# Layer 1's convolution along w: six quarter-width products for four columns in place of four half-width products for two, and another order of the first stage's end

## The chip, the cores and the metric

The kernel runs on one core of one Trainium2 chip, a single launch. The metric is the device time of the whole launch in microseconds. The core's engines work at the same time and wait for each other through semaphores: TensorE (PE, matrix products; PEld is its loading of weights), VectorE (DVE), ScalarE (ACT), GpSimd (POOL) and SyncE (SP, here only the issue of DMAs). Each engine does its instructions in the order in which the program gave them to it.

## The reference

A batch of 8192 images of 8 channels, 16 x 16 pixels, goes through four residual layers, each on a group-normalised input (four groups of two channels, no affine part):

```python
x = x + L0(gn(x))   # a dense map 2048 -> 2048 in tensor-train form, rank 8, plus bias
x = x + L1(gn(x))   # 3x3 convolution, padding 1, plus bias; batch norm over all images; relu
x = x + L2(gn(x))   # 3x3 convolution of a quantised input (+-127, scale from the maximum over everything)
x = x + L3(gn(x))   # 3x3 convolution with binarised weights, edge padding
```

What matters here is layer 1's convolution. For an output column w it is the sum over three taps k of g_k applied to input column w + k - 1. Each g_k is a 128 x 128 matrix, since channels and rows of the image (8 x 16) lie on the 128 partitions and the taps along h are built into a banded matrix.

## The kernel before, in words

**Tiles and stages.** An image batch is cut into NT = 64 tiles of P = 128 images. A tile is 128 partitions (channel, row) by 2048 elements (image, column), 1 MB in float32. There are three stages: the first does layer 0, the norm behind it and layer 1's convolution, the second layer 1's batch norm, relu and residual and the statistics of layer 2, the third layers 2 and 3. The change touches the first stage alone.

**A step.** The first stage is a loop of 256 steps; step n is quarter q = n mod 4 (32 images, 512 columns) of tile t = n div 4. `main(t, q, ...)` does layer 0's main product of the quarter: eight products `po<-u,core` of 512 columns that accumulate in one PSUM buffer, and then DVE's eviction `xs<-po`, which adds the result to x. Between the eight products (at r = 0 to 7) it calls the work that a dictionary `steps` lists for that r, in the order in which it was put in:

- r = 0 and r = 4: `expand` for the next quarter, 16 small products `pu<-w,xn` and ACT's copy `u<-pu` of 2048 elements. There is one `pu` buffer and two `u`.
- r = 1: `conv1_output` of the convolution done at the end of the step before, then `conv1_input` of the one that is done at the end of this step. The convolution runs LAG = 6 steps behind the main product.
- by the quarter: q = 0, `norm_sums(t - 1)` and at r = 4 ACT's squares for a coming tile; q = 1, `norm_stats(t - 1)` at r = 1, and at r = 4 `norm_spread` and `norm_apply` of t - 1; q = 2, `norm_b_sums` and `norm_b_stats`; q = 3, `add_bias` (POOL, 4.5 us) and `norm_b_spread`, `norm_b_apply`.

After `main`, `conv1` does the products of the convolution. So PE's order in a step is `pu`, half of `po`, `pu`, the other half of `po`, `pm`, `pc`.

**The norm chain.** `norm_stats` is a few small DVE instructions (the last is `mv<-mv,sq_a`), and then one on POOL, `mv<-mv,mhalf`, which takes the power -1/2. `norm_spread` is DVE's transpose `stat<-mv`; `norm_apply` is four DVE instructions of 1024 elements that write `x1n`, the normalised input of the convolution, with a zero column on either side.

**The convolution.** Per quarter, with d0 to d3 the four columns under two outputs, `conv1_input` makes d0 - d2 and d1 - d3 (one POOL instruction of 512 elements), d1 + d2 and d2 - d1 (two of 256). `conv1` does four products of 256 columns into `pm` and `pc`, and ACT copies the first half of `pm`, with the bias, into `m`. `conv1_output` makes the two output columns in `y` with three DVE instructions, and `conv1_stats` takes their mean and variance. `conv1_direct` does the last tile with three products of 512 columns a quarter.

**Buffers.** `po`, `pm` and `pc` go round three PSUM buffers with one tag ("mm"), in this order, one each per step. So a step's `po` writes the buffer of the step before's `po`, which `xs<-po` must have read. `v`, the convolution's input, has two buffers.

**Order.** The order on each engine is that of the program (`InOrder`, line 33, through which all of these instructions are recorded; they all bear line 43 in the profile, and are told apart by the names of what they write).

Of the kernel before, what the change touches and what calls it, by code (L numbers as in the profile page):

```python
# [8 lines left out]
F32 = mybir.dt.float32  # L9
# [3 lines left out]
AF = mybir.ActivationFunctionType  # L13
ALU = mybir.AluOpType
# [4 lines left out]
P = 128  # L19
C, H, W = 8, 16, 16  # L20
# [33 lines left out]
def tile_net(ctx: ExitStack, tc: tile.TileContext, xb, xt_in, pack0, pack1, out):  # L54
# [80 lines left out]
    def late_constants(late):  # L135

        w = load_pack(pack1, PACK1, late, "w1")
        yield "load"

        def band(wr, sh, dtype, name):  # L140

            acc = late.tile([P, 3 * C, H], F32, name=f"acc_{name}", tag="acc")
            b = (const1 if name == "1" else const).tile([P, 3, CH], dtype, name=f"band_{name}", tag=f"band_{name}")
            bv = b.rearrange("p k (c h) -> p (k c) h", c=C)
            wr = wr.rearrange("p (k n) -> p k n", k=3)
            for kh in range(3):
                wv = wr[:, kh, :].unsqueeze(2).to_broadcast([P, 3 * C, H])
                mv = sh[:, kh:kh + H].unsqueeze(1).to_broadcast([P, 3 * C, H])
                if kh == 0:
                    dve.tensor_tensor(acc, wv, mv, ALU.mult)  # L150
                    continue
                tmp = late.tile([P, 3 * C, H], F32, name=f"tmp_{name}_{kh}", tag="tmp")
                dve.tensor_tensor(tmp, wv, mv, ALU.mult)
                dve.tensor_tensor(bv if kh == 2 else acc, acc, tmp, ALU.add)
            L[f"band{name}"] = b

        for k in ("gamma", "beta", "bias2", "bias3"):
            L[k] = const.tile([P, 1], F32, name=k)
            dve.tensor_copy(L[k], w[k])

        L["grp"] = grp = blocks(32, 1.0 / 512, "grp")
        b1 = L["b1"] = const.tile([P, 1], F32, name="b1")
        dve.tensor_reduce(b1, w["linb"], AX.X, ALU.add)
        band(w["w1"], shz, F32, "1")

        g0, g1, g2 = (L["band1"][:, k] for k in range(3))
        fast = L["fast1"] = const1.tile([P, 4, CH], F32, name="fast1")
        dve.tensor_tensor(fast[:, 0], g0, g2, ALU.add)
        for k, op in ((1, ALU.add), (2, ALU.subtract)):
            dve.tensor_tensor(fast[:, k], fast[:, 0], g1, op)  # L170
            dve.tensor_scalar(fast[:, k], fast[:, k], 0.5, None, ALU.mult)
        dve.tensor_copy(fast[:, 0], g0)
        dve.tensor_scalar(fast[:, 3], g2, -1.0, None, ALU.mult)
        yield "layer 1"
        L["avg16"] = square_blocks(16, 1.0 / (16 * NT), "avg16")


        w2max = const.tile([P, 1], F32, name="w2max")
        dve.tensor_reduce(w2max, w["w2all"], AX.X, ALU.max, apply_absolute_value=True)
        sw = L["sw"] = const.tile([P, 1], F32, name="sw")  # L180
        dve.reciprocal(sw, w2max)
        dve.tensor_scalar(sw, sw, 127.0, None, ALU.mult)
        wr2 = w["w2"]
        dve.tensor_scalar(wr2, wr2, sw, MAGIC, ALU.mult, ALU.add)
        dve.tensor_scalar(wr2, wr2, MAGIC, 127.0, ALU.subtract, ALU.min)
        dve.tensor_scalar(wr2, wr2, -127.0, None, ALU.max)
        yield "layer 2"
        band(wr2, shz, BF16, "2")
        yield "band 2"


        dve.tensor_copy(she[:, 1:H + 1], shz[:, 1:H + 1])
        dve.tensor_copy(she[:, 0:1], shz[:, 1:2])
        dve.tensor_copy(she[:, H + 1:H + 2], shz[:, H:H + 1])
        wr3 = w["w3"]
        mean3 = L["mean3"] = const.tile([P, C], F32, name="mean3")
        dve.tensor_reduce(mean3, w["w3all"].rearrange("p (o n) -> p o n", o=C), AX.X, ALU.add,
                          apply_absolute_value=True)
        dve.tensor_scalar(mean3, mean3, 1.0 / (C * 9), None, ALU.mult)
        own = blocks(16, 1.0, "own")  # L200
        dve.tensor_tensor(own, own, mean3, ALU.mult)
        scale3 = L["scale3"] = const.tile([P, 1], F32, name="scale3")
        dve.tensor_reduce(scale3, own, AX.X, ALU.add)
        pos3 = late.tile([P, 9 * C], F32, name="pos3")
        dve.tensor_scalar(pos3, wr3, 0.0, None, ALU.is_gt)
        dve.tensor_scalar(wr3, wr3, 0.0, None, ALU.is_lt)
        dve.tensor_tensor(wr3, pos3, wr3, ALU.subtract)
        yield "layer 3"
        band(wr3, she, F32, "3")
        sign3 = L["sign3"] = const.tile([P, 3, CH], F32R, name="sign3")  # L210
        dve.tensor_copy(sign3, L["band3"])
        yield "band 3"

        wsum = L["wsum"] = const.tile([P, 2, 32], F32, name="wsum")
        dve.memset(wsum, 0.0)
        dve.tensor_copy(wsum[:, 0, 0:G], grp)
        dve.tensor_copy(wsum[:, 1, G:2 * G], grp)
        mod32 = const.tile([P, 32], F32, name="mod32")  # L220
        dve.tensor_reduce(mod32, ident.rearrange("p (q j) -> p j q", j=32), AX.X, ALU.add)
        quarter = L["quarter"] = blocks(32, 1.0, "quarter")
        gpad = L["gpad"] = const.tile([P, NQ, 32], F32, name="gpad")
        dve.memset(gpad, 0.0)
        dve.tensor_copy(gpad[:, :, 0:G], quarter.unsqueeze(1).to_broadcast([P, NQ, G]))
        for k, name in enumerate(("sel0", "sel1", "corr")):

            t = L[name] = const.tile([P, CH], F32, name=name)
            dve.tensor_copy(t.rearrange("p (g n) -> p g n", g=G),
                            mod32[:, G * k:G * k + G].unsqueeze(2).to_broadcast([P, G, CH // G]))  # L230
        yield "statistics"
# [16 lines left out]
    def samples(t):  # L248
        return t.rearrange("p (b w) -> p b w", w=W)
# [29 lines left out]
    with first as s:  # L279
# [112 lines left out]

        def conv1_input(t, q):
            x = x1n[t % 2][:, q * QS:(q + 1) * QS]
            v = wk.tile([P, 2, BANK], F32, name=f"v_{t}_{q}", tag="v")
            d, v12 = (v[:, i].rearrange("p (k b j) -> p k b j", k=2, j=W // 2) for i in range(2))
            d1, d2 = x[:, :, 1:W + 1:2], x[:, :, 2:W + 2:2]
            pool.tensor_tensor(d.rearrange("p k b j -> p b j k"),  # L400
                               *(x[:, :, i:i + W].rearrange("p b (j k) -> p b j k", k=2) for i in (0, 2)), ALU.subtract)
            pool.tensor_tensor(v12[:, 0], d1, d2, ALU.add)
            pool.tensor_tensor(v12[:, 1], d2, d1, ALU.subtract)
            T[t]["v", q] = d, v12

        def conv1(t, q):
            d, v12 = T[t].pop(("v", q))
            pm, po = (ps_m.tile([P, 2, BANK // 2], F32, name=f"{n}_{t}_{q}", tag="mm") for n in ("pm", "pc"))
            for ps, v, weights in ((pm, v12, (1, 2)), (po, d, (0, 3))):
                for k in range(2):  # L410
                    pe.matmul(ps[:, k], L["fast1"][:, weights[k]], v[:, k].rearrange("p b j -> p (b j)"),
                              start=True, stop=True)
            m1 = wk.tile([P, BANK // 2], F32, name=f"m1_{t}_{q}", tag="m1")
            act.activation(m1, pm[:, 0], AF.Identity, bias=L["b1"], scale=1.0)
            T[t]["m", q] = m1, pm, po

        def conv1_direct(t, q):

# [18 lines left out]
        def conv1_output(t, q):  # L437
            if q == 0:
                conv1_start(t)
            m1, pm, po = T[t].pop(("m", q))  # L440
            y = T[t]["y"][:, q * BANK:(q + 1) * BANK]
            pairs = [a.rearrange("p (b j) -> p b j", j=W // 2) for a in (m1, pm[:, 1])]
            for k, op in ((0, ALU.add), (1, ALU.subtract)):
                dve.tensor_tensor(samples(y)[:, :, k:W:2], *pairs, op)
            y3 = y.rearrange("p (n k) -> p n k", k=2)
            dve.tensor_tensor(y3, y3, po.rearrange("p k n -> p n k"), ALU.add)
            conv1_stats(t, q)

        def quarter_of(n, lag):
# [96 lines left out]
        norm_sums(t, NQ - 1)  # L546
        if NT > STAY + 2:
            load2(STAY + 2)
        conv1_input(t - 1, 3)
        norm_stats(t)  # L550
        conv1_output(t - 1, 2)
        conv1(t - 1, 3)
        norm_spread(t)
        conv1_start(t)
        for h in range(2):
            norm_apply(t, [h])
            for q in (2 * h, 2 * h + 1):
                conv1_direct(t, q)
            if h == 0:
                conv1_output(t - 1, 3)  # L560
        for q in range(NQ):
            conv1_stats(t, q)

# [410 lines left out]
```

## Time and profile before

| what | value |
|---|---|
| median of 3 runs | 4120.65 us (4120.42 to 4121.55) |
| the profiled execution's own time | 4119.56 us |
| its span, first to last instruction | 4117.4 us |
| PE, PEld busy | 3874.6 us (94%), 2022.6 us (49%) |
| DVE, ACT, POOL busy | 3223.0 us (78%), 2147.3 us (52%), 2047.1 us (50%) |
| mean granted clock of PE | 0.962 |
| 1000 to 2000 us: PE, DVE, ACT, POOL busy | 1000.0, 736.8, 460.9, 338.3 us |

Busy is the time in which an engine had an instruction under way. A product of float32 stands in the trace as two records, so four products of a quarter are eight records of `pm` and `pc`. The last row is a stretch in the middle of the first stage, which ends near 2900 us. Idle time is put down to the engine and the tile that ended it. The granted clock is the share of TensorE's full speed that the chip's throttle let it have.

### The profile page before, as it was taken

To read this page: it belongs to the slowest core of one execution; us is meant where nothing else is said; L and a number is where in the kernel's file an instruction comes from. 1 tells how busy PE (TensorE), PEld (TensorE's weight loads), DVE (VectorE), ACT (ScalarE), POOL (GpSimd) and SP (SyncE) were. 2 spreads that over 40 slices of the span, in tenths; PEclk is the share of its full clock that TensorE was granted. 3 is DMA by queue.
4 is the path that set the end of the run, shared out by engine and by line. 5 is a ranking of instruction groups with operands and counts; after the bars stand their busy time and mean duration, and the time that the engine had idled before them with its cause. 6 is when DMAs were issued, how large, how long until landed. Compare 5 with 4: busy or idle time off the path is not lost.

```text
span 4117.4 us, 50426 instructions
## 1 busy us (share of the span) xinstructions
PE 3874.6 (94%) x19362; PEld 2022.6 (49%) x19362; DVE 3223.0 (78%) x5040; ACT 2147.3 (52%) x1670; POOL 2047.1 (50%) x1350
## 2 busy tenths in 40 slices
PE   7999999999999999999999999999666559999999
PEld 4555555555555555555555555555222125555555
DVE  8777777777777777777777777776799889999997
ACT  4444444444444444444444444443565557777776
POOL 2433333333333333333333333332788759999999
PEclk9999999999999999999999999999777679999999
DMA  3222222222222222222222222211799914444432
GB/s 132 103 82 103 95 91 103 91 94 95 90 103 84 101 103 82 103 100 85 103 92 93 100 87 100 89 75 70 310 425 425 425 79 182 180 183 184 184 154 103
DMA packets 77424, 564.13 MB, mean 137 GB/s; under 512 B 8576, under 2 KB 8704, under 8 KB 8832
## 3 DMA queue, kind: packets, MB, share of 16 engines
q1 hardware_dynamic: 76896, 559.97, 34.9%
q8 instruction: 152, 2.49, 0.2%
q10 hardware_dynamic: 288, 0.94, 0.1%
q14 instruction: 88, 0.72, 0.1%
HBM read 314.47 MB, written 246.42 MB: 136 GB/s over the span
## 4 chain that ended last, share of the span: by engine, by line
PE 86%; DVE 7%; DMA 4%; issue 2%; POOL 1%; ACT 0%; POOLq 0%; DVEq 0%; SPq 0%; ACTq 0%
PE po L43 44%; PE pu L43 13%; PE pf L43 9%; PE pm L43 5%; PE pc L43 5%; PE pq L43 4%; PE s L43 3%; DVE top L43 2%; DMA yk<-y_d 1%; DMA x_d<-u 1%; DMA u<-x_d 1%; DMA x_d<-xs 0%; DMA xs<-x_d 0%; DVE xn L43 0%; POOL xs L43 0%
## 5 line engine op out<-in xcount | busy, mean ns | idle before, releaser
L43 PE MATMUL po<-u,core 128*128 128x512 f32 (+1 forms) x4112 | 1897.7, 604 | 0.0
L43 ACT COPY u<-pu 128x2048 f32<-128x2048 f32 x512 | 955.0, 1865 | 1000.0 <-PE pu L43 1000.0
L43 PEld LDWEIGHTS po<-u,core 128*128 128x128 f32 x4112 | 740.6, 190 | 904.3 <-issue 901.8
L43 POOL TENSOR_TENSOR v<-x1n 128x512 f32<-128x512 f32 x756 | 553.3, 785 | 509.2 <-PE pc L43 291.4
L43 PE MATMUL pu<-w,xn 32*128 32x256 f32 x8192 | 588.6, 401 | 14.3 <-ACT u L43 10.2
L43 PEld LDWEIGHTS pu<-w,xn 32*128 32x128 f32 x8192 | 370.9, 184 | 306.4 <-issue 197.1
L43 POOL TENSOR_TENSOR mv<-mv,mhalf 128x4 f32<-128x4 f32 x128 | 130.3, 1018 | 785.7 <-DVE mv L43 785.7
L43 DVE TENSOR_TENSOR xs<-po,xs 128x512 f32<-128x512 f32 x256 | 176.3, 689 | 393.3 <-PE po L43 393.3
L43 ACT ACTIVATE m<-pm,b 128x256 f32<-128x256 f32 x252 | 119.2, 473 | 547.0 <-PE pm L43 540.8
L43 POOL TENSOR_TENSOR mvb<-mvb,mhalf 128x4 f32<-128x4 f32 x64 | 65.1, 1017 | 607.3 <-DVE mvb L43 607.3
L43 DVE TENSOR_TENSOR ys<-m,pm 128x256 f32<-128x256 f32 x480 | 180.6, 420 | 153.1 <-ACT m L43 153.0
L43 POOL TENSOR_TENSOR xs<-xs,w 128x2048 f32<-128x2048 f32 x64 | 290.9, 4545 | 0.0
L43 PE MATMUL pc<-v,fast 128*128 128x256 f32 x1008 | 258.7, 379 | 2.4 <-DVE bs L43 2.4
L43 PE MATMUL pm<-v,fast 128*128 128x256 f32 x1008 | 258.7, 379 | 0.0
L43 PEld LDWEIGHTS pm<-v,fast 128*128 128x128 f32 x1008 | 191.5, 190 | 133.1 <-issue 119.8
L43 PE MATMUL pf<-hi,sign 128*128 128x512 f32 x768 | 227.0, 433 | 0.0
L43 PE MATMUL pf<-lo,sign 128*128 128x512 f32 x768 | 220.5, 424 | 2.1 <-ACT lo L43 2.0
L43 ACT ACTIVATE sq<-xs 128x2048 f32<-128x2048 f32 (+1 forms) x107 | 199.0, 1860 | 15.0 <-DVE xs L43 10.3
L43 PEld LDWEIGHTS pc<-v,fast 128*128 128x128 f32 x1008 | 191.4, 190 | 28.8 <-issue 2.8
L43 PE MATMUL gb<-rows_c,sel 128*128 128x128 f32 x128 | 40.7, 412 | 169.6 <-DVE rows_c L43 169.6
L43 PE MATMUL pq<-q,band 128*128 128x480 bf16 (+1 forms) x768 | 191.6, 387 | 6.8 <-ACT q L43 3.9
L43 DVE TENSOR_REDUCE s<-sq 128x64 f32<-128x1024 f32 (+1 forms) x130 | 150.5, 1198 | 49.8 <-ACT sq L43 49.7
(237 smaller groups left out, 5807.5 us busy)
## 6 DMA issues: line engine op xcount, KB each, us to landing
x_d<-xs SPq DMA_DIRECT2D x76, 1024.0 KB, 3.9
bs<-in_xb SPq DMA_DIRECT2D x64, 1024.0 KB, 4.9
xs<-in_xt SPq DMA_DIRECT2D x64, 1024.0 KB, 4.9
y_d<-ys SPq DMA_DIRECT2D x60, 1024.0 KB, 3.8
u<-x_d SPq DMA_DIRECT2D x36, 1024.0 KB, 6.3
xs<-x_d SPq DMA_DIRECT2D x32, 1024.0 KB, 8.9
yk<-y_d SPq DMA_DIRECT2D x29, 1024.0 KB, 19.8
bs<-x_d SPq DMA_DIRECT2D x25, 1024.0 KB, 5.2
```

The costliest lines, as they stand in the source:

```text
L43: return self.tc.keep_in_program_order(op(*args, **kwargs))
```

## The change

The convolution along w now makes four output columns at once from six products a quarter of the width (128 columns) each, on six combinations of six neighbouring input columns. Six combined weight matrices are built once, in `late_constants`, with scratch space in `ys[1]` in place of tiles of their own. `conv1_input` has two ACT instructions first (4 and 2 times the input, `x4` of 512 and `x2` of 256 elements) and then eight on POOL (`e` of 512 elements, `r` and four planes of `v` of 128 each, the last two planes of `v` together 256). `e`, `r`, `x2` and `x4` have one buffer each. `conv1` has six products, and two ACT instructions that copy planes 0 (with the bias) and 2 of `pm` into `m`. `conv1_output` has seven DVE instructions: two of 256 elements (one writes back into `pm`), four of 128 that write the four columns, and one of 256 that adds `pc`. At the end of the stage the last tile's statistics and spread stand ahead of the outputs of the tile before it, and those outputs and its last convolution stand between the four direct convolutions of the last tile.

```diff
-        fast = L["fast1"] = const1.tile([P, 4, CH], F32, name="fast1")
-        dve.tensor_tensor(fast[:, 0], g0, g2, ALU.add)
-        for k, op in ((1, ALU.add), (2, ALU.subtract)):
-            dve.tensor_tensor(fast[:, k], fast[:, 0], g1, op)
-            dve.tensor_scalar(fast[:, k], fast[:, k], 0.5, None, ALU.mult)
-        dve.tensor_copy(fast[:, 0], g0)
-        dve.tensor_scalar(fast[:, 3], g2, -1.0, None, ALU.mult)
+        fast = L["fast1"] = const1.tile([P, 6, CH], F32, name="fast1")
+        for k, (f2, f1, f) in enumerate(((1.0, 1.0, -1.0 / 6), (4.0, 2.0, 1.0 / 24))):
+            even = scratch[:, k * CH:(k + 1) * CH]
+            dve.scalar_tensor_tensor(even, g2, f2, g0, ALU.mult, ALU.add)
+            for i, sign, scale in ((2 * k, f1, f), (2 * k + 1, -f1, (-f if k else f))):
+                dve.scalar_tensor_tensor(fast[:, i], g1, sign, even, ALU.mult, ALU.add)
+                dve.tensor_scalar(fast[:, i], fast[:, i], scale, None, ALU.mult)
+        dve.tensor_scalar(fast[:, 4], g0, 0.25, None, ALU.mult)
+        dve.tensor_copy(fast[:, 5], g2)
...
         def conv1_input(t, q):
             x = x1n[t % 2][:, q * QS:(q + 1) * QS]
-            v = wk.tile([P, 2, BANK], F32, name=f"v_{t}_{q}", tag="v")
-            d, v12 = (v[:, i].rearrange("p (k b j) -> p k b j", k=2, j=W // 2) for i in range(2))
-            d1, d2 = x[:, :, 1:W + 1:2], x[:, :, 2:W + 2:2]
-            pool.tensor_tensor(d.rearrange("p k b j -> p b j k"),
-                               *(x[:, :, i:i + W].rearrange("p b (j k) -> p b j k", k=2) for i in (0, 2)), ALU.subtract)
-            pool.tensor_tensor(v12[:, 0], d1, d2, ALU.add)
-            pool.tensor_tensor(v12[:, 1], d2, d1, ALU.subtract)
-            T[t]["v", q] = d, v12
+            e, r, x2, x4 = (wk.tile([P, n, QS, W // 4], F32, name=f"{k}_{t}_{q}", tag=k, bufs=1)
+                            for k, n in (("e", 4), ("r", 2), ("x2", 2), ("x4", 4)))
+            v = wk.tile([P, 6, QS, W // 4], F32, name=f"v_{t}_{q}", tag="v")
...
+            d = x[:, :, 0:W].rearrange("p b (j k) -> p b j k", k=4)
+            act.activation(by_k(x4), d, AF.Copy, scale=4.0)
+            act.activation(by_k(x2), d[:, :, :, 1:4:2], AF.Copy, scale=2.0)
+            pool.tensor_tensor(by_k(e), x[:, :, 2:W + 2].rearrange("p b (j k) -> p b j k", k=4), by_k(x4), ALU.subtract)
+            pool.tensor_tensor(r[:, 0], x2[:, 1], x2[:, 0], ALU.subtract)
+            pool.tensor_tensor(r[:, 1], x[:, :, 4:W + 1:4], d[:, :, :, 2], ALU.subtract)
+            pool.tensor_tensor(v[:, 0], e[:, 2], e[:, 1], ALU.add)
+            pool.tensor_tensor(v[:, 1], e[:, 2], e[:, 1], ALU.subtract)
+            pool.tensor_tensor(v[:, 2], r[:, 1], r[:, 0], ALU.add)
+            pool.tensor_tensor(v[:, 3], r[:, 1], r[:, 0], ALU.subtract)
+            pool.tensor_tensor(v[:, 4:6], e[:, 2:4], e[:, 0:2], ALU.subtract)
+            T[t]["v", q] = v.rearrange("p i b j -> p i (b j)")
...
         def conv1(t, q):
-            d, v12 = T[t].pop(("v", q))
-            pm, po = (ps_m.tile([P, 2, BANK // 2], F32, name=f"{n}_{t}_{q}", tag="mm") for n in ("pm", "pc"))
-            for ps, v, weights in ((pm, v12, (1, 2)), (po, d, (0, 3))):
-                for k in range(2):
-                    pe.matmul(ps[:, k], L["fast1"][:, weights[k]], v[:, k].rearrange("p b j -> p (b j)"),
-                              start=True, stop=True)
-            m1 = wk.tile([P, BANK // 2], F32, name=f"m1_{t}_{q}", tag="m1")
-            act.activation(m1, pm[:, 0], AF.Identity, bias=L["b1"], scale=1.0)
-            T[t]["m", q] = m1, pm, po
+            v = T[t].pop(("v", q))
+            pm, po = (ps_m.tile([P, k, NC], F32, name=f"{n}_{t}_{q}", tag="mm") for n, k in (("pm", 4), ("pc", 2)))
+            for ps, at in ((pm, 0), (po, 4)):
+                for k in range(ps.shape[1]):
+                    pe.matmul(ps[:, k], L["fast1"][:, at + k], v[:, at + k], start=True, stop=True)
+            m = wk.tile([P, 2, NC], F32, name=f"m_{t}_{q}", tag="m")
+            act.activation(m[:, 0], pm[:, 0], AF.Identity, bias=L["b1"], scale=1.0)
+            act.copy(m[:, 1], pm[:, 2])
+            T[t]["m", q] = m, pm, po
...
         def conv1_output(t, q):
...
-            for k, op in ((0, ALU.add), (1, ALU.subtract)):
-                dve.tensor_tensor(samples(y)[:, :, k:W:2], *pairs, op)
-            y3 = y.rearrange("p (n k) -> p n k", k=2)
-            dve.tensor_tensor(y3, y3, po.rearrange("p k n -> p n k"), ALU.add)
+            dve.tensor_tensor(sd, m, pm[:, 1:4:2], ALU.add)
+            dve.tensor_tensor(pm[:, 1:4:2], m, pm[:, 1:4:2], ALU.subtract)
+            s1, d3, d1, s3 = sd[:, 0], sd[:, 1], pm[:, 1], pm[:, 3]
+            y = T[t]["y"][:, q * BANK:(q + 1) * BANK].rearrange("p (n k) -> p k n", k=4)
+            dve.tensor_tensor(y[:, 0], s1, s3, ALU.add)
+            dve.scalar_tensor_tensor(y[:, 1], d3, 2.0, d1, ALU.mult, ALU.add)
+            dve.scalar_tensor_tensor(y[:, 2], s3, 4.0, s1, ALU.mult, ALU.add)
+            dve.scalar_tensor_tensor(y[:, 3], d3, 8.0, d1, ALU.mult, ALU.add)
+            dve.tensor_tensor(y[:, 0:4:3], y[:, 0:4:3], po, ALU.add)
             conv1_stats(t, q)
...
+        norm_stats(t)
         conv1_input(t - 1, 3)
-        norm_stats(t)
-        conv1_output(t - 1, 2)
-        conv1(t - 1, 3)
         norm_spread(t)
         conv1_start(t)
         for h in range(2):
             norm_apply(t, [h])
-            for q in (2 * h, 2 * h + 1):
-                conv1_direct(t, q)
+            conv1_direct(t, 2 * h)
+            conv1_output(t - 1, 2 + h)
+            conv1_direct(t, 2 * h + 1)
             if h == 0:
-                conv1_output(t - 1, 3)
+                conv1(t - 1, 3)
```

More of the change, by code (lines that the diff above doesn't have):

```diff
@@ L138, in late_constants @@
         yield "load"
+        scratch = ys[1]
         def band(wr, sh, dtype, name):
-            acc = late.tile([P, 3 * C, H], F32, name=f"acc_{name}", tag="acc")
+            acc, tmp = (scratch[:, k * 3 * CH:(k + 1) * 3 * CH].rearrange("p (k h) -> p k h", h=H) for k in range(2))
             b = (const1 if name == "1" else const).tile([P, 3, CH], dtype, name=f"band_{name}", tag=f"band_{name}")
@@ L151, in band @@
                     continue
-                tmp = late.tile([P, 3 * C, H], F32, name=f"tmp_{name}_{kh}", tag="tmp")
                 dve.tensor_tensor(tmp, wv, mv, ALU.mult)
@@ new lines, in conv1_input, with by_k @@
+            v = wk.tile([P, 6, QS, W // 4], F32, name=f"v_{t}_{q}", tag="v")
+            def by_k(t):
+                return t.rearrange("p k b j -> p b j k")
+            d = x[:, :, 0:W].rearrange("p b (j k) -> p b j k", k=4)
[3 more added lines that the diff above has]
+            pool.tensor_tensor(r[:, 0], x2[:, 1], x2[:, 0], ALU.subtract)
@@ new lines, in tile_net @@
+        NC = BANK // 4
+        def conv1(t, q):
+            v = T[t].pop(("v", q))
[7 more added lines that the diff above has]
+            T[t]["m", q] = m, pm, po
@@ L439, in conv1_output @@
                 conv1_start(t)
-            m1, pm, po = T[t].pop(("m", q))
-            y = T[t]["y"][:, q * BANK:(q + 1) * BANK]
-            pairs = [a.rearrange("p (b j) -> p b j", j=W // 2) for a in (m1, pm[:, 1])]
-            for k, op in ((0, ALU.add), (1, ALU.subtract)):
-                dve.tensor_tensor(samples(y)[:, :, k:W:2], *pairs, op)
-            y3 = y.rearrange("p (n k) -> p n k", k=2)
-            dve.tensor_tensor(y3, y3, po.rearrange("p k n -> p n k"), ALU.add)
+            m, pm, po = T[t].pop(("m", q))
+            sd = wk.tile([P, 2, NC], F32, name=f"sd_{t}_{q}", tag="sd")
+            dve.tensor_tensor(sd, m, pm[:, 1:4:2], ALU.add)
[7 more added lines that the diff above has]
+            dve.tensor_tensor(y[:, 0:4:3], y[:, 0:4:3], po, ALU.add)
             conv1_stats(t, q)
```

## The prediction

> **What bounds the kernel now.** I read the page's busy slices first, then stretches of the first stage, then one tile of it in order of time. Seven tenths of the span are the first stage (0 to 2900 us), and there, from the second slice on, TensorE is all but never idle, at full clock:
>
> ```profile
> PE   7999999999999999999999999999666559999999
> ...
> PEclk9999999999999999999999999999777679999999
> ```
>
> In stretches, the columns being length, busy time (and count) of PE, PEld, DVE, ACT, POOL, then granted clock, DMA share and GB/s:
>
> ```profile
> 1000.00:2000.00 1000.00, 1000.00 (x5022) 524.32 (x5021) 736.81 (x1098) 460.89 (x316) 338.25 (x335) 1.00 0.25 95
> ```
>
> So PE sets the pace here, and time taken from it is gained, unless another chain then holds it up. The instructions in order of time (start, length, engine) give the chain nearest to doing so. This is the step with q = 1 of one tile; S = 1505.78 is the start of its first expansion:
>
> ```profile
> 1494.85 2.20 POOL L43 TENSOR_TENSOR v<-x1n 128x512 f32<-128x512 f32 x3 [4.51 <-PE pc L43]
> ...
> 1505.78 1.15 PE L43 MATMUL pu<-w,xn 32*128 32x256 f32 x16
> ...
> 1507.04 1.86 ACT L43 COPY u<-pu 128x2048 f32<-128x2048 f32 x1 [1.49 <-PE pu L43]
> ...
> 1509.34 1.02 POOL L43 TENSOR_TENSOR mv<-mv,mhalf 128x4 f32<-128x4 f32 x1 [12.29 <-DVE mv L43]
> ...
> 1510.39 0.46 DVE L43 STREAM_TRANSPOSE stat<-mv 128x256 f32<-128x256 f32 x1 [1.13 <-POOL mv L43]
> ...
> 1510.88 1.22 DVE L43 TENSOR_TENSOR x1n<-xs,stat 128x1024 f32<-128x1024 f32 x1
> ...
> 1515.66 0.68 DVE L43 TENSOR_TENSOR xs<-po,xs 128x512 f32<-128x512 f32 x1
> ...
> 1516.91 1.15 PE L43 MATMUL pu<-w,xn 32*128 32x256 f32 x16
> ...
> 1517.99 3.70 PE L43 MATMUL po<-u,core 128*128 128x512 f32 x8
> ```
>
> The reader is to see four things. A step is 11.14 us (1505.77 to 1516.91), a tile four steps, 44.56. The POOL triple at 1494.85 is this step's `conv1_input`, done a whole step early. Hence POOL stands idle for 12.29 us before its one-microsecond power, and starts that at S+3.56. Behind it on DVE, with no idle, come the spread, four `norm_apply` instructions and then the eviction `xs<-po`, which ends at 1516.34. The next main product writes that same PSUM buffer (`po`, `pm`, `pc` go round three), at 1517.99: a slack of 1.65 us.
>
> **What the Trainium skill says.** "TensorE: Matmul & The Clock Gate", Part 1 (The HAM clock gate), says that PE falls to half clock after an idle window of about 3.4 us and returns after a busy one. This trace shows it, and more sharply. Stretches of 3.41 us after 2914 us, cut where the clock changes (PE busy, clock, DMA share, GB/s):
>
> ```profile
> 2972.17:2975.58 3.41, 1.39 (x12) 1.00 1.01 408
> 2975.58:2978.99 3.41, 3.41 (x18) 0.50 1.02 430
> 2978.99:2982.40 3.41, 1.76 (x20) 1.00 1.01 425
> 2982.40:2985.82 3.42, 1.00 (x12) 1.00 1.00 422
> 2985.82:2989.23 3.41, 2.54 (x12) 0.50 1.02 423
> 2989.23:2992.64 3.41, 2.23 (x12) 0.50 1.01 425
> ```
>
> After 1.39 us busy the clock is halved, after 1.76 it is not; one full stretch restores it, 2.54 us do not. Others of this cut give 1.63 (halved) and 1.82 (not). So about 1.7 us of idle inside one stretch halves the next. "GPSIMD Engine Reference", section 3.1, gives about 2.6 cycles per element of a two-input operation, some twice DVE's cost; the rows below agree ((1113 - 621)/256 = 1.92 ns). "TensorE: Matmul & The Clock Gate", LDWEIGHTS, says a load takes time by its columns, not its rows: at 128 moving columns a product is then no longer than its load, which I price from the trace.
>
> **The change on PE.** The only 128-column products back to back at full clock are three, two records each, at 2899.91; their loads:
>
> ```profile
> 2899.91 0.30 PEld L640 LDWEIGHTS kps<-band,gpad 128*128 128x128 f32 x2 [0.40 <-issue]
> 2900.35 0.41 PEld L640 LDWEIGHTS kps<-band,gpad 128*128 128x128 f32 x2
> ```
>
> The first and the fifth load start 0.44 us apart: 0.11 us per record, loads overlapped although each lasts 0.19. The present 256-column records follow at 0.2155 (1504.171 to 1504.387). A quarter goes from 8 x 0.2155 = 1.72 to 12 x 0.11 = 1.32 us: 0.40 less, and 252 x 0.40 = **-101 us** if nothing else moves. The step becomes 10.74 us.
>
> **The other engines.** Rows by form (count | busy, mean ns):
>
> ```profile
> L43 POOL TENSOR_TENSOR v<-x1n 128x256 f32<-128x256 f32 x504 | 301.8, 621 | 0.0
> L43 POOL TENSOR_TENSOR v<-x1n 128x512 f32<-128x512 f32 x252 | 280.4, 1113 | 509.2 <-PE pc L43 291.4 <-DVE x1n L43 199.9 <-issue 17.9
> L43 DVE TENSOR_TENSOR ys<-m,pm 128x256 f32<-128x256 f32 x480 | 180.6, 420 | 153.1 <-ACT m L43 153.0
> L43 ACT ACTIVATE sq<-xs 128x512 f32<-128x512 f32 x4 | 2.5, 626 | 0.0
> ```
>
> POOL goes from three instructions (2.19 us, with starts 1.00 and 0.58 apart) to eight: one of 512, six of 128, one of 256. No row has 128; the line through 512 and 256 gives 0.37 apart. Sum 1.00 + 6 x 0.37 + 0.62 = **3.84 us**. Ends: 2.5 if an instruction costs nothing beside its 1536 elements (0.42/256 ns each), 5.1 if a 128 costs as much as a 256. ACT gains `x4` (0.63) and `x2` (about 0.41), and two `m` of about 0.37 for one of 0.47: +1.3 per quarter, 5.2 per tile on 20.5 of 43; hidden by its waits for PE. DVE's output goes from 1.54 us to 2.0-2.4 (two of 256 starting 0.34 apart, four of 128 at 0.20 to 0.29, one of 256): 2 to 3.6 us more per tile on 32.8 of 43, hidden by its waits for `po` and, at q = 1, for the power. Were that cover gone, the statistics would be ready at S+4.9 at the latest, still no bound by themselves.
>
> **The wait that appears.** `conv1_input` now begins with two ACT instructions, and ACT takes them in order, behind `u` of the same step. POOL can no longer run a step ahead. And at q = 1 `norm_stats`, with POOL's power, is issued behind `conv1_input`. So, from S: `u` ends at 3.12; `x4` ends at 3.76; POOL begins at 3.80, ends its eight at 7.64; the power starts at 7.69, not 3.56. From the power's start to the end of the eviction is 7.00 us (1509.34 to 1516.34) and does not change: 14.69. With 0.08 for the signal the next main product starts at 14.77. PE could have started it at 12.21 - 0.40 = 11.81. It stalls **2.96 us**, once a tile. Queued behind the power on DVE are spread, apply, eviction, the next outputs and `norm_b_sums`; these end near S+24, before their own deadline of about S+25.5, so the delay dies out within the tile. At the other steps `v` is ready at 7.64 and its first load is due at 8.90: no stall, 1.26 to spare. Tiles concerned: t = 2 to 63, 62. Cost 62 x 2.96 = **+184 us**. A tile of 42.97 + 2.96 = 45.9 is already longer than 44.56.
>
> **And the clock.** A gap of 2.9 us on a grid of 3.41 leaves 1.7 us idle in one stretch unless a boundary falls into its middle 0.5 us: 85% of tiles. Each halved stretch of a busy PE loses 1.71; where the gap reaches more than some 0.6 us into the next stretch there are two. I take 1.8 x 0.85 = 1.5 us a tile: 62 x 1.5 = **+93 us**; bounds 0 and 1.8.
>
> **What costs nothing.** Twelve DVE instructions of about 0.25 us instead of eight build the weights: 1 us once, beside the first tile's work; `scratch` in `ys[1]` moves no work. At the end of the stage power and spread come ahead of the output of t - 1, which leads DVE about 1.4 us sooner to `x1n`, but seven-instruction outputs follow: -1, between -4 and +4. No DMA is added or moved.
>
> **Sum.** -101 + 184 + 93 + 0 = +176. The profiled execution took 4119.56 us with a span of 4117.4; the median of the runs is 4120.65. Forecast 4120 + 175 = **4295**.
>
> **Rivals.**
> - *The stall without the clock*: PE stays at full clock, since the gap is just short of a stretch. For it: 200 to 2850 us show clock 1.00 throughout, with no gap to judge by. Against it: the stretches above. 4120 - 101 + 184 = 4203.
> - *Faster*: the power is not late. It decides at a POOL set of 2.5 us, where the stall is 1.6, all that four quarters gain. For it: that is the lower price above. Against it: 256 elements take 0.58 today. With no stall, 4020.
> - *Weights bound PE*: if each 0.19 us load stood unhidden, 12 x 0.19 = 2.28, +0.56 a quarter, +141 beside the stall. Against it: the 0.11 above. About 4500.
> - *`v` late in every step*: with a POOL set above 5.1 us PE waits four times a tile and the q = 1 stall passes 4.2. Above 4380.
>
> **How the numbers follow.** Stall and clock 0.60 (POOL 3.3 to 4.3 us: 4235 to 4340), stall alone 0.20 (4165 to 4235), faster 0.10, no change 0.02 (within 0.2%, which is about what a measurement here can tell from none), the last two rivals and worse 0.08. The range reaches from 4190, taking in most of the second case, to 4345. Faster 0.10, same 0.02, slower 0.88.
>
> **What would show it.** In the profile after: `pm` and `pc` records 0.11 apart; eight POOL instructions of `conv1_input` starting after `u` and `x4`; the row of the power with much less idle before it and started behind them; PE idle before `po`, released by DVE `xs`, about 62 times near 3 us; PEclk below 1 in the first 28 slices, and stretches at 0.50 behind those gaps. Wrong it would be if POOL's 128-element instructions cost under 0.15 us apart, or if `po` shows no idle.

## The result and the profile after

The changed kernel takes 4432.27 us (4430.45 to 4433.22), the kernel before in the same comparison 4121.1 us: a ratio of 1.0754 (1.0736 to 1.0773), 311 us more. The forecast was 4295 with a range of 4190 to 4345. Direction and place were right, the size was not. The profiled execution took 4433.22 us, with a span of 4431.4; the last main product of the first stage starts at 3184.9 us, against 2872.9, so the whole difference arises there.

PE's busy tenths and its granted clock in the page's 40 slices:

```profile
PE   7998999899989999899989998999856658999999
...
PEclk9999999999999999999999999999877669999999
```

PE is no longer full from slice to slice. A stretch in the middle of the stage (length, then busy time and count of PE, PEld, DVE, ACT, POOL, then granted clock, DMA share, GB/s):

```profile
1000.00:2000.00 1000.00, 918.59 (x4860) 487.59 (x4859) 782.28 (x1313) 530.74 (x527) 517.40 (x709) 0.95 0.23 87
```

PE now stands idle for 8% of the time, and its clock is 0.95 where it was 1.00. No other engine is near full, which speaks for a chain of waits and against a load. The chain, in order of time, at one step with q = 1 (S, the start of its first expansion, is 1512.38):

```profile
1512.38 1.15 PE L43 MATMUL pu<-w,xn 32*128 32x256 f32 x16
...
1513.59 1.86 ACT L43 COPY u<-pu 128x2048 f32<-128x2048 f32 x1 [1.03 <-PE pu L43]
...
1515.35 1.56 ACT L43 ACTIVATE x<-x1n 128x512 f32<-128x512 f32 x2
...
1516.60 1.57 POOL L43 TENSOR_TENSOR e<-x1n,x 128x512 f32<-128x512 f32 x1 [5.99 <-ACT x L43]
...
1521.27 1.02 POOL L43 TENSOR_TENSOR mv<-mv,mhalf 128x4 f32<-128x4 f32 x1
...
1522.32 0.46 DVE L43 STREAM_TRANSPOSE stat<-mv 128x256 f32<-128x256 f32 x1 [3.32 <-POOL mv L43]
...
1523.13 1.15 PE L43 MATMUL pu<-w,xn 32*128 32x256 f32 x16
...
1527.60 0.68 DVE L43 TENSOR_TENSOR xs<-po,xs 128x512 f32<-128x512 f32 x1
...
1528.34 6.71 PE L43 MATMUL po<-u,core 128*128 128x512 f32 x8 [4.06 <-DVE xs L43]
```

(`x` in the names is `x4` and `x2`, since the profile leaves numbers out.) Before, POOL did its triple a step ahead and stood idle 12.29 us before the power; now it waits 5.99 us for ACT before `e`, and the power follows without any idle, behind the eight. DVE waits 3.32 us for the power, and PE 4.06 us for DVE's eviction of `po`. Then the same eight records of `po` take 6.71 us, not 3.70. Two stretches show what lies around that point, the first without work for PE, the second from the start of these records on:

```profile
1524.30:1528.30 4.00, 0.00 (x0) 0.00 (x0) 3.97 (x5) 3.32 (x3) 0.95 (x1) 0.91 0.18 47
1528.34:1534.98 6.64, 6.64 (x9) 2.53 (x9) 6.43 (x12) 0.00 (x0) 3.72 (x8) 0.54 0.69 287
```

PE had four microseconds without work, and in the 6.64 that follow its clock is 0.54. It happens in every tile. The view of waits from 200 to 2800 us (what waited for whom: us in total, times, longest) has

```profile
PE po L43 <- DVE xs L43: 212.0, 52, 4.3
```

that is, a gap of 4.08 us on average in each of the 52 tiles there. A tile takes 49.49 us from one `norm_spread` to the next, 44.56 before: 62 x 4.93 = 306 of the 311 us.

### The profile page after: what moved, and what is told of

Read it like the earlier page. It is cut to its first block, busy times and chain, and to the rows that moved or that the text cites. A ratio compares the mean times of both kernels' runs of the same rounds, so it can differ in the third digit from the quotient of the medians.

```text
span 4431.4 us, 55604 instructions
## 1 busy us (share of the span) xinstructions
PE 3929.3 (89%) x20308; PEld 2070.2 (47%) x20370; DVE 3587.0 (81%) x6053; ACT 2516.3 (57%) x2426; POOL 2687.9 (61%) x2610
## 4 chain that ended last, share of the span: by engine, by line
PE 65%; DVE 13%; POOL 8%; issue 5%; ACT 4%; DMA 4%; POOLq 0%; DVEq 0%; SPq 0%; ACTq 0%
PE po L43 34%; PE pu L43 9%; PE pf L43 9%; DVE x1n L43 5%; PE pm L43 4%; PE pq L43 4%; POOL v L43 3%; ACT u L43 3%; PE s L43 3%; DVE top L43 2%; PE pc L43 2%; POOL mv L43 1%; ACT x L43 1%; DVE xs L43 1%; POOL r L43 1%
## 5 line engine op out<-in xcount | busy, mean ns | idle before, releaser
L43 PE MATMUL po<-u,core 128*128 128x512 f32 (+1 forms) x4112 | 2045.9, 644 | 255.3 <-DVE xs L43 255.3
L43 PEld LDWEIGHTS po<-u,core 128*128 128x128 f32 x4112 | 793.8, 203 | 1251.6 <-issue 908.3
L43 POOL TENSOR_TENSOR e<-x1n,x 128x512 f32<-128x512 f32 x252 | 396.6, 1574 | 1178.3 <-ACT x L43 1172.2
L43 POOL TENSOR_TENSOR v<-e 128x128 f32<-128x128 f32 x756 | 404.0, 549 | 0.0
L43 ACT ACTIVATE m<-pm,b 128x128 f32<-128x128 f32 x252 | 92.5, 367 | 536.2 <-PE pm L43 399.6
L43 ACT ACTIVATE x<-x1n 128x512 f32<-128x512 f32 x504 | 395.8, 887 | 1.3 <-POOL e L43 1.3
L43 PEld LDWEIGHTS pm<-v,fast 128*128 128x128 f32 x2016 | 264.7, 191 | 121.6 <-issue 119.3
L43 PE MATMUL pm<-v,fast 128*128 128x128 f32 x2016 | 266.4, 275 | 0.3 <-DVE bs L43 0.3
L43 DVE TENSOR_TENSOR sd<-m,pm 128x256 f32<-128x256 f32 x252 | 105.5, 418 | 144.3 <-ACT m L43 144.3
L43 POOL TENSOR_TENSOR v<-r 128x128 f32<-128x128 f32 x504 | 219.7, 459 | 0.0
```

Of the source, the lines that this page charges most:

```text
L43: return self.tc.keep_in_program_order(op(*args, **kwargs))
```

## The experiments

My theory had three parts. First, the power of q = 1 is late because it stands behind POOL's new work, which itself stands behind ACT's `u`. Second, PE pays for it at the `po` buffer. Third, the gap (PE's idle time there) halves the clock afterwards. Rivals were that all engines simply have too much to do, that 128-column products are dearer than 0.11 us, and that the order at the end of the stage matters. Times below are to be held against 4121 and 4432 us. Those of e1, e9 and e10 are medians of four runs, the others single runs; four runs of one kernel lay within 5 us of each other. PE's gaps (over 0.3 us), the stretches at half clock and the tile lengths are counted in the traces between 200 and 2800 us. In e1, e5, e9 and e10 the first stage ends inside that stretch, and its end is left out of them.

### e1: the statistics first

In the program `at(r, condition, f, ...)` puts a call of `f` into the list for r, and `at1` does so for the convolution's functions. At q = 1 `norm_stats` now comes first in the list for r = 1, ahead of `conv1_output` and `conv1_input`.

```diff
+                at(1, q == 1 and before, norm_stats, t - 1)
                 at1(1, conv1_output, LAG + 1)
                 at1(1, conv1_input, LAG)
...
             elif q == 1:
-                at(1, before, norm_stats, t - 1)
+                at(1, n == NT * NQ - 1 and before, norm_stats, t - 1)
```

> The changed kernel, with the statistics of the norm (norm_stats, DVE and then POOL's power) issued first in the step with q = 1, ahead of conv1_output and conv1_input; nothing else is moved. My theory (the power stands behind conv1_input's eight POOL instructions, the delay ends in the main product's wait for its PSUM buffer, and that wait halves the clock): power at about S+1, no wait of po for DVE xs, clock 1.00 in the whole steady first stage, a tile 42.98 us, time 4020 to 4030. Rival (DVE, ACT and POOL have too much to do in a step, wherever the power stands): the tile stays at 47 us or more, time above 4300. Rival (128-column products cost PE more than 0.11 us a record): no waits, but above 4060.

Measured: 4029.37 us (4027.56 to 4030.28), ratio to the kernel before 0.9778 (0.9762 to 0.9795). A tile is 43.00 us, four steps of 10.75; there is no gap before any `po`. The same stretch as above, in this kernel:

```profile
1000.00:2000.00 1000.00, 1000.00 (x5582) 541.02 (x5581) 861.27 (x1515) 610.73 (x606) 592.27 (x814) 1.00 0.26 98
```

Nothing was taken away: DVE, ACT and POOL do all of the change's work, now 86%, 61% and 59% busy, and PE is full at full clock. So the load is not the cause, and neither are the products. One call's place in a list is worth 403 us here. This version beats both kernels.

### e2: only the power ahead of POOL's eight

Here `norm_stats` stands behind `conv1_output` and ahead of `conv1_input`.

```diff
                 at1(1, conv1_output, LAG + 1)
+                at(1, q == 1 and before, norm_stats, t - 1)
                 at1(1, conv1_input, LAG)
...
             elif q == 1:
-                at(1, before, norm_stats, t - 1)
```

> The changed kernel, with norm_stats at q = 1 behind conv1_output but ahead of conv1_input: the same DVE order as the change, only POOL's power and its eight instructions change places. My theory: power at about S+5.1 (when DVE has mv), eviction over at S+12.1, so po waits 0.3 to 0.4 us; the eight POOL instructions end near S+10.7, so the last products of pm and pc wait up to 0.5 us; no halved clock; about 4055 (4035 to 4075). Rival (too much work, not the order): above 4300.

Measured: 4074.27 us, a tile 43.73. DVE's order is that of the change; only POOL's is turned round. The gap before `po` is gone and the clock stays full. What I expected for `v` came: the loads of `pm` and `pc` wait for POOL's `v` in 59 tiles, by up to 0.3 and 0.4 us. So POOL's order alone carries 358 of the 403 us. The trace of e2 shows where e1's further 45 us come from: its step with q = 1 takes 11.47 us and the other three 10.75, as all four do in e1, and the excess lies behind the start of `pm`, where the loads wait for `v`. That is 0.72 us a tile, and 62 x 0.72 = 45. In e1 DVE has the statistics earlier, so the power goes before POOL's work is due and delays no `v`.

### e3, e11, e12, e4: ACT's position, and a dose

In e3 `conv1_input` of q = 1 is called ahead of `expand`, so ACT's two instructions stand before `u`; the power remains behind the eight.

```diff
+        EARLY = (1,)
...
+            if n < NT * NQ - 1 and q in EARLY:
+                at1(0, conv1_input, LAG)
             at(0, tn < NT, expand, tn, qn, 0)
...
-                at1(1, conv1_input, LAG)
+                if q not in EARLY:
+                    at1(1, conv1_input, LAG)
```

The others do this too, and put m further POOL instructions of 128 elements behind the eight of that step (m = 1, 2, 3 in e11, e12, e4), which write the same values once more. The step with q = 1 prepares quarter 3 of an earlier tile, hence the `q == 3`:

```diff
+            for _ in range(m if q == 3 else 0):
+                pool.tensor_tensor(r[:, 1], x[:, :, 4:W + 1:4], d[:, :, :, 2], ALU.subtract)
             T[t]["v", q] = v.rearrange("p i b j -> p i (b j)")
```

> The changed kernel, with conv1_input at q = 1 called at r = 0 ahead of expand, so that its two ACT instructions stand ahead of the copy u, not behind it; the power still stands behind the eight POOL instructions. My theory: e starts at S+1.4 in place of S+4.2, the power at S+6.1 in place of S+8.9, the wait of po shrinks from 4.1 to 1.3 us a tile, under the 1.7 us that halve the clock: clock 1.00, tile 44.3 us, about 4106. If the clock falls all the same: about 4230. Rival (ACT's position does not matter): 4432.

> The kernel of e4 with one extra POOL instruction in place of three: gap of PE about 1.67 us a tile, just at the 1.7 us of idle in a stretch of 3.41 that I read from the profile before. My theory: half-clock stretches after few or none of the gaps (0 to 20%), 4130 to 4150. If the threshold were lower (1.3 us): after more than half of them, above 4180.

> The same with two extra instructions: gap about 2.15 us, over the threshold if it lies in one stretch. Stretches of 3.41 us cut it so that 1.7 us stay in one in about (3.41 - 2.15 + 2 x 0.45) / 3.41 = 63% of tiles: clock loss about 1.0 us a tile, 4210 to 4235. If the threshold were 2.2 us or more: no half clock, 4160.

> The kernel of e3 with one of the 128-element POOL instructions of q = 1 done three times more (the same values into the same place), a dose of 3 x 0.41 = 1.24 us ahead of the power. My theory: wait of po 2.6 us a tile; most of these gaps halve a stretch of the clock, some 1.4 us lost a tile; about 4270. If only the wait counts and the clock stays: 4183. If POOL's position ahead of the power does not matter: as e3.

Measured: 4106.14, 4135.38, 4212.74 and 4286.24 us. The waits of PE in e3 and in e4:

```profile
PE po L43 <- DVE xs L43: 70.7, 59, 1.5
```

```profile
PE po L43 <- DVE xs L43: 146.2, 55, 2.9
```

All that was counted in these traces, with e1 as the zero, and with e6 (below) and the change:

| kernel | gap of PE, us a tile | half clock, us a tile | gaps followed by half clock | tile, us | more than e1 |
|---|---|---|---|---|---|
| e1 | 0 | 0 | none | 43.00 | 0 |
| e3 | 1.20 | 0 | 0 of 59 | 44.27 | 1.27 |
| e11 | 1.61 | 0.06 | 1 of 58 | 44.71 | 1.71 |
| e12 | 2.12 | 1.65 | 27 of 56 | 46.01 | 3.01 |
| e4 | 2.66 | 2.67 | 43 of 55 | 47.06 | 4.06 |
| e6 | 3.24 | 3.48 | 54 of 54 | 47.85 | 4.85 |
| the change | 4.08 | 5.12 | 52 of 52 | 49.49 | 6.49 |

In e3 the gap falls from 4.08 to 1.20 us, so ACT's position counts. The first, second and third further instruction delay the power, counted from the start of `e`, by 0.41, 0.53 and 0.53 us, and the gap grows by 0.41, 0.51 and 0.54. So POOL's place ahead of the power acts as supposed, one for one. The clock answers as a threshold does: a gap of 1.20 us costs itself and 0.07 more, and nothing else; 1.61 us does so too; from 2.12 on, half clock comes after a rising share of the gaps.

Where the threshold lies can be read from the same traces. The clock changes on a grid of 3.41 us. Two stretches of that grid in e4, each with the one behind it:

```profile
424.91:428.32 3.41, 1.44 (x4) 0.73 (x5) 3.34 (x9) 2.71 (x3) 1.08 (x1) 1.00 0.65 214
428.32:431.73 3.41, 3.41 (x6) 1.24 (x4) 3.24 (x7) 0.00 (x0) 3.41 (x8) 0.50 0.69 286
...
1131.47:1134.88 3.41, 1.47 (x4) 0.75 (x5) 3.34 (x9) 2.69 (x3) 1.10 (x1) 1.00 0.66 221
1134.88:1138.29 3.41, 3.41 (x23) 1.58 (x22) 3.24 (x7) 0.03 (x1) 3.41 (x8) 1.00 0.67 279
```

With 1.44 us of work in a stretch the next one is halved, with 1.47 it is not. All 111 gaps of e12 and e4, cut on this grid, agree: none of the 41 that leave at most 1.95 us of idle time in any one stretch was followed by half clock, and all 70 that leave 1.97 or more in one were. The single case in e11 was an unusually long gap, 1.89 us in one stretch. So the threshold is some 1.9 us in one stretch of the grid, and a gap of 2.12 us passes it only when no boundary divides it much.

The cost of half clock adds up: e4 has 4.06 - (2.66 + 0.07) = 1.33 us above its gap, and half of 2.67 us at half clock is 1.33. For e12 it is 0.82 and 0.82. In the change it is 2.34 against 2.56, as a part of the halved stretch falls into the gap itself, where there is nothing to slow. There 26 of the 52 halvings last 3.41 us and 26 last 6.83; in e4 all 43 last 3.41. Over 62 tiles the last line of the table comes to 62 x 6.49 = 402, of the 403 us between e1 and the change.

### e5: the products alone

This is the kernel before with six products of 128 columns and all else as it was; `pc`'s second half is not computed.

```diff
-            for ps, v, weights in ((pm, v12, (1, 2)), (po, d, (0, 3))):
-                for k in range(2):
-                    pe.matmul(ps[:, k], L["fast1"][:, weights[k]], v[:, k].rearrange("p b j -> p (b j)"),
+            for ps, v, weights, m in ((pm, v12, (1, 2), 4), (po, d, (0, 3), 2)):
+                ps, v = ps.rearrange("p k n -> p (k n)"), v.rearrange("p k b j -> p (k b j)")
+                for k in range(m):
+                    pe.matmul(ps[:, 128 * k:128 * k + 128], L["fast1"][:, weights[k % 2]], v[:, 128 * k:128 * k + 128],
                               start=True, stop=True)
+            po = po[:, 0:1].to_broadcast([P, 2, BANK // 2])
```

> The kernel before, with six products of 128 columns in conv1 in place of four of 256, and nothing else of the change: POOL, ACT and DVE work as before (pc's second half is not computed, its first half is read twice, so layer 1 is not the reference's). My theory: 0.39 to 0.40 us less a quarter, about 4021, no wait and no halved clock. Rival (loads of weights bound 128-column products): 4121 to 4260.

Measured: 4025.61 us, a tile 43.00. PE's part of the change is worth 93 us, near the 101 of the sum; in the steady stage it is (44.56 - 43.00) / 4 = 0.39 us a quarter, where 0.40 was counted. e1, with the whole change, is within 4 us of it: all the work that the change adds to the other three engines costs almost nothing once PE does not wait for it.

### e6: the order of `x4` in memory

In the change `by_k` puts every fourth column of `x4` together in one plane, so ACT writes `x4`, and POOL reads it for `e`, with a jump from plane to plane at each element. In e6 `x4` keeps the input's own order; `e` is still written in planes.

```diff
-            act.activation(by_k(x4), d, AF.Copy, scale=4.0)
+            x4 = x4.rearrange("p k b j -> p (k b j)").rearrange("p (b j k) -> p b j k", j=W // 4, k=4)
+            act.activation(x4, d, AF.Copy, scale=4.0)
...
-            pool.tensor_tensor(by_k(e), x[:, :, 2:W + 2].rearrange("p b (j k) -> p b j k", k=4), by_k(x4), ALU.subtract)
+            pool.tensor_tensor(by_k(e), x[:, :, 2:W + 2].rearrange("p b (j k) -> p b j k", k=4), x4, ALU.subtract)
```

> The changed kernel, with x4 kept in the input's own order in place of four planes, so ACT writes and POOL's e reads it in one run. It asks why x4 took 1.11 and e 1.57 us where the rows of before led me to 0.63 and 1.10. If the planes are the cause: x4 near 0.63, e near 1.10, the power 0.95 us earlier, wait of po 3.2 us, 4340 to 4385. If it is the size of the work or the traffic of other engines: no change, 4432.

Measured: 4329.14 us. Rows by form (count | busy, mean ns | idle before), first of the change:

```profile
L43 POOL TENSOR_TENSOR e<-x1n,x 128x512 f32<-128x512 f32 x210 | 330.5, 1574 | 969.0 <-ACT x L43 969.0
...
L43 ACT ACTIVATE x<-x1n 128x512 f32<-128x512 f32 x210 | 233.0, 1109 | 0.0
```

then of e6:

```profile
L43 POOL TENSOR_TENSOR e<-x1n,x 128x512 f32<-128x512 f32 x218 | 263.8, 1210 | 996.8 <-ACT x L43 996.8
...
L43 ACT ACTIVATE x<-x1n 128x512 f32<-128x512 f32 x218 | 138.1, 633 | 0.0
```

The planes of `x4` were the cause. With the same elements on the same engines, 1109 becomes 633 ns on ACT, which is near the 626 of the row I had priced it by, and 1574 becomes 1210 on POOL, where the row of before has 1113; that last 0.1 us stays open. The 0.84 us together shorten the gap by 0.84 and the time by 103 us, twice what 62 gaps of 0.84 are, since half clock also goes from 5.12 to 3.48 us a tile.

### e7, e8, e9, e10: controls

e7 is the change with the order of the stage's end as before (the last hunk of the change undone), e8 the kernel before with e1's edit, e9 is e1 with e7's end, e10 is e1 with e6's edit.

> The changed kernel with the order of the first stage's end as before. My theory: the order at the end is worth a few us at most, 4432 within 6 us either way. Rival: it is a visible part of the loss, below 4420.

> The kernel before with norm_stats first at q = 1, as in e1. It is the control: there the power was never late, so 4121 within 4 us. If it is faster by more, part of e1's gain would not come from the change's own wait.

> The kernel of e1 (statistics first at q = 1) with the first stage's end ordered as before. In e1 the stage's end is the one place left where PE waits long (7.1 us before pd). My theory: as in e7, the order at the end is worth 0 to 6 us: 4023 to 4030. Rival: now that the steady stage has no wait, the end decides more: more than 8 us either way.

> The kernel of e1 with x4 in the input's own order, as in e6: ACT and POOL save about 0.9 us a step. My theory: nothing stands behind them any more, so e1's time within 4 us (4025 to 4033), although the same edit was worth 100 us on the changed kernel. Rival (ACT and POOL still bound something): 4000 to 4020.

Measured: e7 4429.92, e8 4117.87 us (4118.58 for the kernel before beside it), e9 4029.85 us (4026.95 to 4031.84; ratio 0.9778, 0.9762 to 0.9794), e10 4027.49 us (4027.24 to 4028.91; ratio 0.9775, 0.9761 to 0.9790). The order at the end makes no difference that can be told, with or without the waits. The statistics' place is worth nothing in the kernel before, so what e1 recovers is the change's own wait. And the edit that was worth 103 us on the change is worth nothing measurable on e1, where it is off the path.

## Why the prediction was right in kind and wrong in size

- **PE's gain** (-101). Right: records of `pm` start 0.111 us apart in the trace after (eight from 1521.70 to 1522.59), a step without a wait is 10.75 us (1512.38 to 1523.13; 10.74 stood in the working), and e5 has 93 us.
- **The chain, its place and its end**. Right, step for step: POOL behind ACT, the power behind POOL's eight, the wait of `po` for DVE, once a tile. From the power's start to the end of the eviction it is 7.01 us (7.00 said). e1 to e4 bear it out.
- **The step that failed is "the wait that appears", in two of its terms.** `x4` was priced at 0.63 us from the squares' row and took 1.11, so `e` started at S+4.22 and not at 3.80. POOL's set was priced at 3.84 us, 3.89 to the power's start, from the line through 256 and 512 elements, and took 4.67 to there (1516.60 to 1521.27): `e` alone 1.52 to the next start, not 1.00, and the 128s 0.41 each, not 0.37. The stall is so 4.13 us (1528.34 against 1523.13 + 1.08) in place of 2.96. That is +73 us over 62 tiles. e6 shows the reason for most of it, 0.84 of 1.17 us: ACT's row was of an instruction that writes in one run and POOL's of one that reads both inputs in one run, and `by_k` makes ACT's output and POOL's input jump between planes. The shape in the row agreed, the access did not, and the range of 2.5 to 5.1 us that I gave for POOL took in the true value but my central figure did not.
- **The clock.** The mechanism held: idle time is counted on a grid of 3.41 us, and enough of it in one stretch halves the next. My threshold of 1.7 us, read from stretches behind the first stage, was somewhat low: the gaps of this stage need some 1.9, and 27 of 56 gaps in e12 were followed by half clock where I expected 63%. The Trainium skill ("TensorE: Matmul & The Clock Gate", Part 1) speaks of a whole idle window of about 3.4 us; here less than two thirds of one was enough. The term failed mainly as it was mis-fed: 1.5 us a tile was for a gap of 2.9, and at 3.24 e6 lost 1.54. At 4.08 it was 2.34, over my bound of 1.8. Every gap of that length halved the clock, and in 26 of 52 so much of it reached into the halved stretch, at least 0.74 us, that the next one was halved as well. That is +52 us over 62 tiles. One size error was thus paid twice. With PE's gain at 93 for 101, the sum is then 176 + 73 + 52 + 8 = 309, of 311 measured.
- **The other terms at nothing.** Right: loads of DVE, ACT and POOL and the building of weights (e1, which has all of them, against e5), and the end of the stage (e7, e9). One reading was off without effect: DVE's statistics, expected at S+4.9 at the latest, were ready at S+6.6, held up beside `e`, which is still before POOL was free for the power at S+8.9.
- **Rivals.** "Weights bound PE" and "`v` late in every step" are out by e5 and e1. "The stall without the clock" is out by the table. "Faster" was put down to a short POOL set, which is out; but its time, 4020, is near what another place for the power gives, 4029 in e1.

## What to carry to other kernels

When work is moved to an engine, ask first what is queued behind it there and who waits for that, even for a one-microsecond instruction on an engine that is 34% busy; a reorder may then be worth more than the arithmetic. A row lends its duration only to instructions with the same access as well as the same shape. And a wait of the matrix engine can have two prices: in this kernel up to 1.9 us it cost itself, and longer ones, the more surely the longer, half clock besides.

## What was not expected of the hardware

- Plane-wise access has a price: at 512 elements a scaled copy on ACT took 1.11 us with its output in planes and 0.63 without, a two-input instruction on POOL 1.57 with one input in planes and 1.21 without (e6).
- In the change a DVE instruction of eight elements takes eight times its usual time where POOL's `e` runs:

```profile
1516.78 1.42 DVE L43 TENSOR_SCALAR mv<-mv 128x8 f32<-128x8 f32 x1
```

It ends at 1518.20, `e` at 1518.17. Before and in e1 it takes 0.171 us on average, in e6, where `e` ends sooner, 0.593, and in e3, beside POOL's 128-element instructions, 0.176. The next two on DVE (`sq_a<-mv` and `mv<-mv,sq_a`, two inputs each) do slow down beside those short ones: 0.39 and 0.37 us in the change, 0.34 and 0.38 in e3, against 0.16 before and in e1. The Trainium skill ("GPSIMD Engine Reference", 1. Specifications) says that POOL shares its memory interfaces with DVE, and that DVE instructions in a two-port mode or with two inputs from SBUF can collide with it. The two-input ones fit that; what held up the eight-element one behind `e` was not tried. It cost nothing here, since the power waited for POOL anyway.
- DVE's 128-element outputs took 0.39 us, and the last of 256 took 0.63, where rows of before had 0.29 and 0.42; a whole output was 2.67 us to the start of its statistics, where 2.0 to 2.4 was forecast. It is off the path in e1.
